# Attention probabilities turned by VectorE in 32x32 blocks, and a context product in four row tiles of 32 partitions

## The chip, the core and the metric

The kernel runs on one core of one Trainium2 chip. The metric is device time in microseconds, from the start to the end of one execution; of the kernel before there are three runs, and their median is what the prediction is compared with. A profiled execution gives every instruction's start, duration and releaser. Engines are named as in the profile: PE (matrix products; PEld is its weight load), DVE (VectorE), ACT (ScalarE), POOL (GpSimd) and SP, which here only issues transfers.

## The reference

The model is a gated two-layer block over x of 4 batches x 512 rows x 512. Layer 0 has a learned sparse adjacency over the context (top 153 of 512 per row) and a ternary feed-forward network behind a Hadamard transform. Layer 1 has the attention that this change touches, and a second ternary feed-forward network. The attention, cut to what matters (16 heads, 512 queries, 512 keys, latent width 128):

```python
q_big = rope(einsum('bshk,hkq->bshq', (hidden_q @ Wq.T), w_kc_q))
kv_r  = rope(kv_c)                                     # 512 x 128 per batch, for all heads
q_r   = einsum('bshq,hqr->bhsr', q_big, W_qr)
k_r   = einsum('bld,hdr->bhlr', kv_r, W_kr)
attn  = softmax(einsum('bhsr,bhlr->bhsl', q_r, k_r))   # 512 x 512 per head
ctx_c = einsum('bhsl,bld->bhsd', attn, kv_r)           # the context product
ctx   = einsum('bhsd,hkd->bhsk', ctx_c, w_kc_kv)       # folded with Wo into one matrix per head
out   = ctx @ Wo.T
```

## The kernel before

The kernel has three stretches. In the first (to about 286 us) it prepares the first batch's adjacency and feed-forward network, makes weights ternary, and `ahead` (lines 694-727) computes things for later: the rotated context `kv[b]` of every batch, which stays on chip as [128 keys of a chunk, 4 chunks, 128], and per head the folded matrix `om`, kept in DRAM. The middle stretch is `attention` (917-954): 4 batches x 8 pairs of heads, 32 pairs. In the last stretch the second feed-forward network of the last batch ends the kernel.

A pair runs in four quarters j = 0..3, one for each 128 queries. In a quarter, `scores(j)` makes for both heads the score tile [128 queries, 512 keys] (PE, lines 863 and 866, in 64 partitions each), its row maximum (DVE, 871), the exponentials with row sums (ACT, 874), the reciprocal (DVE, 876) and the normalized tile `pp` (ACT, 877). The next pair's queries are made in the same quarters: `head` (804), `rope` (819, with DVE 827, 829, 832 and POOL 833), and after the last quarter `rotated` (790, 792, in two column halves).

`turn(j)` (880-886) turns probabilities: for each head four PE transposes of 128x128 (885) into one PSUM bank `ppt`, then one ACT copy (886) into `pT`. It is called two quarters late, the last two after the quarters. Then `attended` (888-899) makes the context product: per head four accumulating products of `kv` (weights, 128 keys x 128) with `pT` (128 keys x 512 queries), and an ACT copy (898) to `cxo`. `added` (901-910) multiplies `cxo` with the two heads' `om` (905) for each 128 queries, and DVE adds the result to x (910). In fp32 the profile shows two PE instructions for each such product, and one for each transpose.

Other work is woven between the quarters. After each quarter, the loop at the end (1029-1051) takes steps of a list of jobs until their planned costs reach the share that is due: for batches 1 to 3 `before(b)`, which holds the adjacency of the next batch (the top-k by repeated MAX8, line 486, and MATCH_REPLACE8, line 491, on DVE), the keys of the next batch, and its first feed-forward network; in the last batch, the second network's weights and the second networks of batches 0 to 2. The top-k steps are given a priority 800 places behind (`high_priority(offset=-FILL)`, 483 and 488), so that they fill DVE where attention leaves room. Every engine works through its own list in a fixed order, made when the program is built; transfers are issued by SP and POOL, also in order.

PSUM has eight banks: four `mm` for products, two `tr` for transposes, two `bg` for the woven work. The on-chip tiles of this change are `pT` (two buffers of [128, 4, 512], one for each head), `pp` (seven), and `cxo` (three).

Of the kernel before, what the change touches and what calls it, by code (L numbers as in the profile page):

```python
# [9 lines left out]
F32 = mybir.dt.float32  # L10
# [24 lines left out]
def flamingo_kernel(  # L35
# [18 lines left out]
    wp = ctx.enter_context(tc.tile_pool(name="attn", bufs=2))  # L54
    ps = ctx.enter_context(tc.tile_pool(name="ps", bufs=4, space=bass.MemoryType.PSUM))
    pst = ctx.enter_context(tc.tile_pool(name="pst", bufs=2, space=bass.MemoryType.PSUM))
    psb = ctx.enter_context(tc.tile_pool(name="psb", bufs=2, space=bass.MemoryType.PSUM))

    def mm_ps(name):
        return ps.tile([P, 512], F32, tag="mm", name=name)  # L60

    def tr_ps(name):
        return pst.tile([P, 4, P], F32, tag="tr", name=name)


    alone = [True]
    turn_of = {"tr": 0, "big": 0, "front": 0}

# [10 lines left out]
    def bg_tr(name, dt=F32):  # L79
        if mine("tr", 4):  # L80
            return psb.tile([P, 4, P], dt, tag="bg", name=name)
        return pst.tile([P, 4, P], dt, tag="tr", name=name)

# [15 lines left out]

    lent = []  # L100

    def big(name):
        place = lent.pop(0) if lent else None
        if place == "h":
            t = hp.tile([P, NC, S], F32, tag="hT", name=name, bufs=1)
            return t.rearrange("p c s -> p (c s)")
        if place == "t":
            t = wp.tile([P, NT, S], F32, tag="pT", name=name)
            return t.rearrange("p j s -> p (j s)")
        if place == "b":  # L110
            return bp.tile([P, FF], F32, tag="big", name=name, bufs=3)
        turn_of["big"] += 1
        if not alone[0] or turn_of["big"] % 5 in (1, 3, 0):
            return bp.tile([P, FF], F32, tag="big", name=name, bufs=3)
        t = wp.tile([P, NT, S], F32, tag="pT", name=name)
        return t.rearrange("p j s -> p (j s)")

# [574 lines left out]
    spilled = {}  # L692

    def ahead():

# [7 lines left out]
        for b in range(B):  # L703
            cb = wp.tile([P, NT, DC], F32, tag="qh", name=f"cb_{b}")
            nc.gpsimd.dma_start(cb, cx[b * S : (b + 1) * S, :].rearrange("(j p) d -> p j d", p=P))
            t = const.tile([P, NT, DC], F32, tag=f"kv{b}", name=f"kv_{b}")
            nc.gpsimd.tensor_tensor(t, cb, cos_k, ALU.mult)
            rt = wp.tile([P, NT, DC], F32, tag="rs", name=f"rt_{b}", bufs=3)
            nc.gpsimd.tensor_tensor(rt[:, :, :hf], cb[:, :, hf:], sin_k[:, :, :hf], ALU.mult)
            nc.gpsimd.tensor_tensor(rt[:, :, hf:], cb[:, :, :hf], sin_k[:, :, hf:], ALU.mult)  # L710
            nc.gpsimd.tensor_tensor(t, t, rt, ALU.add)
            kv[b] = t
        yield
        for h in range(NH):
            wv = hp.tile([P, DC], F32, tag="wk", name=f"wv_{h}", bufs=3)
            nc.sync.dma_start(wv, wkckv[h])
            wo = wp.tile([P, D], F32, tag="rs", name=f"wo_{h}", bufs=3)
            nc.sync.dma_start(wo, woT[h])
            po = mm_ps(f"pO_{h}")
            nc.tensor.matmul(po, wv, wo, start=True, stop=True)  # L720
            om = wp.tile([P, D], F32, tag="cxo", name=f"oms_{h}", bufs=3)
            nc.scalar.copy(om, po)
            d = dram.tile([P, D], F32, tag=f"om{h}", name=f"omd_{h}")
            nc.gpsimd.dma_start(d, om)
            om_d[h] = d
            yield
        yield from keys(0)

    def keys(b):

        pt = bg_tr(f"pkv_{b}")
        for j in range(NT):
            nc.tensor.transpose(pt[:, j, :], kv[b][:, j, :], ident)

# [3 lines left out]
        for g in range(NG):  # L738
# [4 lines left out]
            if alone[0]:  # L743
                k = wp.tile([P, S], F32, tag="cxo", name=f"krs_{b}_{g}", bufs=3)
            else:
                k = front_t(f"krs_{b}_{g}")
# [47 lines left out]
    class Pair:  # L794
# [41 lines left out]
        def rotated(self):  # L836
# [5 lines left out]
            for o in range(3):  # L842
# [7 lines left out]
            nc.scalar.copy(self.qr, pr)  # L850
            self.pT = [
                wp.tile([P, NT, S], F32, tag="pT", name=f"pT_{u}_{i}") for i in range(2)
            ]

# [24 lines left out]

        def turn(self, j):  # L880
            for i in range(2):
                pt = tr_ps(f"ppt_{self.u}_{i}_{j}")
                pp = self.pps.pop((i, j))
                for l in range(NT):
                    nc.tensor.transpose(pt[:, l, :], pp[:, l * P : (l + 1) * P], ident)  # L885
                nc.scalar.copy(self.pT[i][:, :, j * P : (j + 1) * P], pt)  # L886

        def attended(self):
            self.cxo = []
            for i in range(2):  # L890
                pc = mm_ps(f"pc_{self.u}_{i}")
                for l in range(NT):
                    nc.tensor.matmul(  # L893
                        pc, kv[self.b][:, l, :], self.pT[i][:, l, :],
                        start=(l == 0), stop=(l == NT - 1),
                    )
                cxo = wp.tile([P, S], F32, tag="cxo", name=f"cxo_{self.u}_{i}", bufs=3)
                nc.scalar.copy(cxo, pc)  # L898
                self.cxo.append(cxo)

        def added(self):
            for j in range(NT):
                po = mm_ps(f"po_{self.u}_{j}")
                for i in range(2):
                    nc.tensor.matmul(  # L905
                        po, self.cxo[i][:, j * P : (j + 1) * P], self.oms[i],
                        start=(i == 0), stop=(i == 1),
                    )
# [8 lines left out]
    def attention(first):  # L917


        order = [(b, g) for b in range(B) for g in range(NG)]  # L920
        cur = first
        for at, (b, g) in enumerate(order):
            nxt = begin(*order[at + 1]) if at + 1 < len(order) else None
            cur.oms = out_weights(b, g)
            fresh = nxt is not None and nxt.b != b
            for j in range(NT):
                cur.scores(j)
                if nxt:
# [9 lines left out]
                    else:  # L938
                        nxt.rope(2)
                if j > 1:  # L940
                    cur.turn(j - 2)
                yield b, g
            cur.turn(NT - 2)
            cur.turn(NT - 1)
            if nxt:
                nxt.rotated()
            cur.attended()
            cur.added()
            if g == NG - 1 and b < B - 1:
                for j in range(NT):  # L950
                    d = dram.tile([P, D], F32, tag=f"xd{b}_{j}", name=f"xd_{b}_{j}")
                    nc.sync.dma_start(d, xs[b, j])
                    spilled[b, j] = d
            cur = nxt

# [34 lines left out]
    for _ in f0:  # L990
        step(early, 1)
    drain(early)
    hidden_T(0)
    first.head(0)
# [3 lines left out]
    first.rotated()  # L998
    alone[0] = False

    w1 = []
# [177 lines left out]
```

## Time and profile before

| | |
|---|---|
| runs of the kernel before | 2048.23, 2048.83, 2052.68 us; median 2048.83 us |
| span of the profiled execution | 2048.8 us |
| granted PE clock, mean over the span | 0.960 (0.77 in 0 to 286 us, 0.97 to 1.00 in attention) |
| PE / DVE / ACT / POOL busy | 1819.6 / 1630.3 / 1081.8 / 336.1 us |
| first score product, last `po` product | 286.3 us, 1961.4 us |
| attention batch 0 / 1 / 2 / 3 | 416 / 414 / 422 / 423 us |

The page gives, for each engine, its busy time and share of the span; then groups of equal instructions: line, engine, operation, tiles written and read, shape, count, busy time (overlaps counted once), mean duration of one, and the engine's idle time just before them. Tables by window give busy microseconds of each engine in a stretch of the span, with the number of instructions, and the granted PE clock. A timeline gives start, length, engine, line and operation; consecutive equal instructions are merged into one row with their count. Matrix products overlap in the pipeline, so the distance of two starts tells more than a duration.

### The profile page before, as it was taken

What the parts mean: (1) busy time and instruction counts of PE and PEld (TensorE: products, weight loads), DVE (VectorE), ACT (ScalarE), POOL (GpSimd) and SP (SyncE); (2) the same over time, 40 slices, a digit from 0 to 9 for tenths busy, and PEclk for the clock granted to TensorE, in tenths of its full rate; (3) what the DMA queues carried; (4) which work ended last, traced back from release to release, by engine and by line L of the source; (5) the groups of instructions that cost most, each with busy time, mean ns of one, the idle gap of its engine ahead of it and who ended that gap; (6) DMA issues with size and microseconds to landing.
All of it is one profiled execution on the core that took longest, in us unless ns stands there. A gap on an engine that the chain in (4) does not pass through costs nothing. (4 is left out here: it accounts for less than half of the span.)

```text
span 2048.8 us, 22947 instructions
## 1 busy us (share of the span) xinstructions
PE 1819.6 (89%) x7874; PEld 889.2 (43%) x7874; DVE 1630.3 (80%) x3305; ACT 1081.8 (53%) x1833; POOL 336.1 (16%) x316
## 2 busy tenths in 40 slices
PE   1268799999999999999999999999989999999898
PEld 0035534436554344455444444555443444444333
DVE  7989699987776999977778999778758556866785
ACT  6935454354434455453444564534786565555544
POOL 3020031123011122130111221301111210111000
PEclk6579899999999999999999999999999999999999
DMA  7451021111111222111122121111783112222011
GB/s 269 155 179 38 1 74 45 55 49 28 42 43 48 89 71 72 38 38 37 41 55 84 57 84 47 35 35 38 241 302 128 50 40 74 68 53 67 21 34 39
DMA packets 115556, 151.90 MB, mean 74 GB/s; under 512 B 57456, under 2 KB 68080, under 8 KB 112368
## 3 DMA queue, kind: packets, MB, share of 16 engines
q1 hardware_dynamic: 109968, 134.51, 22.0%
q0 software_dynamic: 4320, 14.16, 1.9%
q10 hardware_dynamic: 1152, 1.77, 0.2%
q8 instruction: 62, 1.02, 0.2%
q14 instruction: 54, 0.44, 0.1%
HBM read 117.90 MB, written 19.92 MB: 67 GB/s over the span
## 5 line engine op out<-in xcount | busy, mean ns | idle before, releaser
L833 POOL TENSOR_TENSOR ro<-ro,rs 128x512 f32<-128x512 f32 x192 | 255.4, 1333 | 1153.3 <-DVE rs L829 648.3
L874 ACT ACTIVATE pp<-pss,nm 128x512 f32<-128x512 f32 x256 | 174.6, 685 | 272.3 <-DVE nm L871 271.5
L804 PE MATMUL pqh<-hT,wq 128*128 128x512 f32 x512 | 239.7, 606 | 6.8 <-ACT pp L874 5.6
L893 PE MATMUL pc<-pT,kv 128*128 128x512 f32 x512 | 236.0, 600 | 2.7 <-ACT pT L886 2.6
L905 PE MATMUL po<-om,cxo 128*128 128x512 f32 x512 | 229.9, 597 | 0.0
L819 PE MATMUL pb<-qh,wc 128*128 128x512 f32 x384 | 189.4, 613 | 13.6 <-ACT qh L809 7.7
L486 DVE MAX8 m<-work 128x8 f32<-128x512 f32 x304 | 198.7, 684 | 0.6
L871 DVE TENSOR_REDUCE nm<-pss 128x1 f32<-128x512 f32 x256 | 167.8, 683 | 38.1 <-PE pss L866 37.9
L491 DVE MATCH_REPLACE8 work<-m,work 128x512 f32<-128x512 f32 x288 | 193.6, 678 | 0.1
L877 ACT ACTIVATE pp<-pp,rsm 128x512 f32<-128x512 f32 x256 | 178.6, 720 | 27.4 <-DVE rsm L876 26.2
L886 ACT COPY pT<-ppt 128x512 f32<-128x512 f32 x256 | 142.1, 588 | 38.5 <-PE ppt L885 38.0
L885 PEld LDWEIGHTS ppt<-ident,pp 128*128 128x128 f32 x1024 | 117.7, 142 | 96.6 <-issue 37.1
L885 PE MATMUL ppt<-ident,pp 128*128 128x128 f32 x1024 | 147.8, 279 | 10.1 <-ACT pp L877 4.4
L910 DVE SCALAR_TENSOR_TENSOR x<-po,gt,x 128x512 f32<-128x512 f32 x128 | 94.8, 745 | 68.4 <-PE po L905 67.6
L804 PEld LDWEIGHTS pqh<-hT,wq 128*128 128x128 f32 x512 | 93.1, 191 | 128.4 <-issue 89.6
L863 PE MATMUL pss<-kr,qr 64*128 64x512 f32 x256 | 143.4, 641 | 4.4 <-ACT pp L874 2.6
L905 PEld LDWEIGHTS po<-om,cxo 128*128 128x128 f32 x512 | 93.9, 190 | 119.5 <-issue 101.2
L866 PE MATMUL pss<-kr,qr 64*128 64x512 f32 x256 | 143.4, 641 | 0.7 <-DVE ro L827 0.5
L827 DVE TENSOR_TENSOR ro<-pb,cos_q 128x512 f32<-128x512 f32 x192 | 130.9, 682 | 10.3 <-PE pb L819 9.5
L893 PEld LDWEIGHTS pc<-pT,kv 128*128 128x128 f32 x512 | 91.9, 190 | 105.0 <-issue 90.4
L819 PEld LDWEIGHTS pb<-qh,wc 128*128 128x128 f32 x384 | 65.6, 189 | 113.6 <-issue 40.9
L898 ACT COPY cxo<-pc 128x512 f32<-128x512 f32 x64 | 37.4, 584 | 145.1 <-PE pc L893 144.8
(279 smaller groups left out, 3062.0 us busy)
## 6 DMA issues: line engine op xcount, KB each, us to landing
wq<-in_wqh SPq DMA_DIRECT2D x64, 256.0 KB, 2.7
om<-omd SPq DMA_DIRECT2D x64, 256.0 KB, 2.8
wc<-in_wkcq SPq DMA_DIRECT2D x32, 384.0 KB, 3.1
krd<-krs POOLq DMA_DIRECT2D x32, 256.0 KB, 2.5
kr<-krd SPq DMA_DIRECT2D x32, 256.0 KB, 2.7
sa_w1v<-in_gvT SPq DMA_DIRECT2D x8, 1024.0 KB, 5.3
sb_w1v<-in_gvT SPq DMA_DIRECT2D x8, 1024.0 KB, 5.2
wr<-in_wqr SPq DMA_DIRECT2D x32, 192.0 KB, 2.4
```

The costliest lines, as they stand in the source:

```text
L486: nc.vector.max(m8[j], cur[j])
L491: nc.vector.match_replace(works[j], m8[j], cur[j], GONE)
L804: nc.tensor.matmul(pq, self.wqs[i][:, c, :], hT[self.b][:, c, :], start=(c == 0), stop=(c == NC - 1),)
L819: nc.tensor.matmul(pb, self.wc[:, at : at + P], self.qhs[i if i < 2 else o], start=True, stop=True)
L833: nc.gpsimd.tensor_tensor(ro, ro, rs, ALU.add)
L863: nc.tensor.matmul(*args, start=True, stop=True)
L871: nc.vector.tensor_reduce(nm, pss[i], AX.X, ALU.max, negate=True)
L874: nc.scalar.activation(pp, pss[i], AF.Exp, bias=nm, accum_out=sm)
L877: nc.scalar.activation(pp, pp, AF.Copy, scale=rs)
L885: nc.tensor.transpose(pt[:, l, :], pp[:, l * P : (l + 1) * P], ident)
L893: nc.tensor.matmul(pc, kv[self.b][:, l, :], self.pT[i][:, l, :], start=(l == 0), stop=(l == NT - 1),)
L905: nc.tensor.matmul(po, self.cxo[i][:, j * P : (j + 1) * P], self.oms[i], start=(i == 0), stop=(i == 1),)
```

## The change

Probabilities are no longer turned on PE. `turn(j)` becomes two DVE instructions, one for each head: each turns the 32x32 blocks of a [128, 512] tile `pp` where they are, into `pT`. So row 32a+i of `pT` now holds key i of every block of 32 keys, for the 32 queries of block a. The keys of one block lie on 32 partitions in four copies (one for each 32 queries a), and the context product becomes, for each group a of 32 partitions, 16 accumulating products over the 16 blocks of 32 keys, with 256 columns (2 heads x 4 quarters x 32 queries). The four groups write four PSUM banks. The weights for this are the context laid out 32 rows at a time and repeated on all four groups: `kvrep`, loaded from DRAM for each batch by four transfers (`values`).

```diff
+    def values(b):
+        t = const.tile([P, 16, DC], F32, tag="kvrep", name=f"kvrep_{b}")
+        rows = kv_d[b].rearrange("(a i) j d -> i j a d", i=32)
+        for g in range(4):
+            nc.sync.dma_start(
+                t[32 * g : 32 * g + 32].rearrange("i (j a) d -> i j a d", j=NT), rows
+            )
+        kv[b] = t
...
         def turn(self, j):
+            if self.pT is None:
+                self.pT = wp.tile([P, 2, NT, S], F32, tag="pT", name=f"pT_{self.u}", bufs=1)
             for i in range(2):
-                pt = tr_ps(f"ppt_{self.u}_{i}_{j}")
-                pp = self.pps.pop((i, j))
-                for l in range(NT):
-                    nc.tensor.transpose(pt[:, l, :], pp[:, l * P : (l + 1) * P], ident)
-                nc.scalar.copy(self.pT[i][:, :, j * P : (j + 1) * P], pt)
+                nc.vector.transpose(self.pT[:, i, j, :], self.pps.pop((i, j)))
 
         def attended(self):
-            self.cxo = []
-            for i in range(2):
-                pc = mm_ps(f"pc_{self.u}_{i}")
-                for l in range(NT):
-                    nc.tensor.matmul(
-                        pc, kv[self.b][:, l, :], self.pT[i][:, l, :],
-                        start=(l == 0), stop=(l == NT - 1),
-                    )
-                cxo = wp.tile([P, S], F32, tag="cxo", name=f"cxo_{self.u}_{i}", bufs=3)
-                nc.scalar.copy(cxo, pc)
-                self.cxo.append(cxo)
+            pcs = [mm_ps(f"pc_{self.u}_{g}") for g in range(4)]
+            for c in range(16):
+                for g in range(4):
+                    rows = slice(32 * g, 32 * g + 32)
+                    with tc.high_priority() if c + g else nullcontext():
+                        nc.tensor.matmul(
+                            pcs[g][:, : 8 * 32], kv[self.b][rows, c, :],
+                            self.pT[rows, :, :, 32 * c : 32 * c + 32].rearrange("p i j s -> p (i j) s"),
+                            start=(c == 0), stop=(c == 15), skip_group_check=True,
+                        )
+            self.cxo = wp.tile([P, 8, 4, 32], F32, tag="cxo2", name=f"cxo_{self.u}", bufs=1)
+            for g in range(4):
+                nc.scalar.copy(self.cxo[:, :, g, :], pcs[g][:, : 8 * 32].rearrange("p (m s) -> p m s", m=8))
...
         for at, (b, g) in enumerate(order):
...
             for j in range(NT):
                 cur.scores(j)
...
-                if j > 1:
-                    cur.turn(j - 2)
+                if j == 0:
+                    if prev:
+                        ended(prev)
+                    cur.oms = out_weights(b, g)
+                cur.turn(j)
                 yield b, g
-            cur.turn(NT - 2)
-            cur.turn(NT - 1)
             if nxt:
                 nxt.rotated()
-            cur.attended()
-            cur.added()
...
-            cur = nxt
+            cur, prev = nxt, cur
+        ended(prev)
```

`ended(p)` calls `attended` and `added`, and at a batch's last pair spills x and calls `values(b + 1)`; it holds what stood at the end of the loop before. So product and addition of a pair stand in the first quarter of the next pair, behind that quarter's scores and query product. `high_priority` holds the 64 products of a pair together on PE.

Further edits: the two `tr` banks join `mm`, which now has six; `pT` is one tile for both heads with one buffer in place of two; `cxo` has one buffer, and the larger `cxo2` is new. `ahead` no longer keeps `kv[b]` on chip, it writes it to DRAM (four transfers on POOL's queue), and `keys(b)` loads it from there (one transfer on SP). Some tiles of the first stretch change their place (`oms`, `krs` in `ro`; the large tiles of `big` use the two halves of `pT`). `values(0)` stands ahead of the first pair.

## Prediction

> **What bounds the kernel now.** I read the busy shares first, then the busy time by stage, then the groups of the lines that go or move, then two stretches of the timeline. The chain of waits reaches back only to 1292 us and gives PE 23%, DVE 7%, ACT 4% of the span: PE leads, mostly with lines 893, 905, 436 and 804.
>
> The table by stage, split where the top-k of the next batch ends (columns: stage, its length, then busy us of each engine with instructions, granted PE clock, share of DMA, GB/s):
>
> ```profile
> core 0: us, PE busy (x) PEld busy (x) DVE busy (x) ACT busy (x) POOL busy (x), PEclk, DMA share, GB/s
> 286.00:452.00 166.00, 158.33 (x502) 67.89 (x502) 161.52 (x355) 80.99 (x162) 32.11 (x27) 1.00 0.17 50
> 452.00:702.00 250.00, 234.75 (x1286) 127.80 (x1284) 189.84 (x341) 111.49 (x210) 42.82 (x40) 0.99 0.17 44
> 702.00:876.00 174.00, 164.64 (x526) 71.54 (x526) 165.45 (x373) 89.31 (x174) 37.63 (x36) 1.00 0.23 69
> 876.00:1116.00 240.00, 228.17 (x1278) 124.19 (x1276) 186.71 (x334) 110.95 (x209) 43.20 (x36) 1.00 0.17 44
> 1116.00:1290.00 174.00, 164.45 (x523) 71.23 (x522) 165.47 (x372) 88.72 (x173) 37.66 (x36) 1.00 0.23 70
> 1290.00:1538.00 248.00, 230.13 (x1274) 127.78 (x1274) 179.74 (x302) 146.75 (x238) 44.19 (x36) 0.97 0.41 135
> 1538.00:1961.00 423.00, 400.92 (x1442) 175.56 (x1439) 286.00 (x576) 239.04 (x399) 54.53 (x42) 0.99 0.23 62
> ```
>
> Each of batches 0 to 2 has two stages of four pairs: a **top-k stage**, in which DVE is busy 95 to 97% and PE 95%, and a **feed stage**, in which PE is busy 93 to 95% and DVE 72 to 78%. Batch 3 (the last row) has no top-k: PE 95%, DVE 68%. So time taken from PE counts in the feed stages and in batch 3, and time added to DVE counts in the top-k stages. ACT is nowhere near the bound.
>
> What the change removes, and what it comes to sit beside, in the groups (columns: line, engine, operation, tiles, shape, count, busy us, mean ns, idle before with its releaser):
>
> ```profile
> L893 PE MATMUL pc<-pT,kv 128*128 128x512 f32 x512 | 236.0, 600 | 2.7 <-ACT pT L886 2.6
> ...
> L871 DVE TENSOR_REDUCE nm<-pss 128x1 f32<-128x512 f32 x256 | 167.8, 683 | 38.1 <-PE pss L866 37.9
> ...
> L886 ACT COPY pT<-ppt 128x512 f32<-128x512 f32 x256 | 142.1, 588 | 38.5 <-PE ppt L885 38.0
> ...
> L885 PE MATMUL ppt<-ident,pp 128*128 128x128 f32 x1024 | 147.8, 279 | 10.1 <-ACT pp L877 4.4 <-ACT pT L886 4.1 <-ACT hT L762 1.5
> ```
>
> **The PE transposes go.** 147.8 us busy and 10.1 us of waits before them, 157.9 us over 32 pairs: 4.9 us a pair off PE. The waits of the product for `pT` (2.7 us in all) go too; I leave them out.
>
> **The context product on PE.** Before, 16 PE instructions of 512 columns a pair; the chain shows sixteen in 7.06 us, and their starts lie 0.43 us apart, so 6.9 us. After, 64 products with two instructions each, 128 of 256 columns. At half of 0.43 us each, 27.5 us if they run one after the other, 6.9 us if four groups of partitions run beside each other. The nearest row is the score product, which already runs in two groups of 64 partitions (timeline of all engines, start and length):
>
> ```profile
> 1537.06 0.59 PE L905 MATMUL po<-om,cxo 128*128 128x512 f32 x1
> 1537.58 0.18 PEld L863 LDWEIGHTS pss<-kr,qr 64*128 64x128 f32 x1 [0.76 <-issue]
> 1537.58 0.69 PE L863 MATMUL pss<-kr,qr 64*128 64x512 f32 x1
> 1537.59 0.18 PEld L866 LDWEIGHTS pss<-kr,qr 64*128 64x128 f32 x1
> 1537.59 0.69 PE L866 MATMUL pss<-kr,qr 64*128 64x512 f32 x1
> ...
> 1538.11 0.59 PE L863 MATMUL pss<-kr,qr 64*128 64x512 f32 x1
> 1538.12 0.59 PE L866 MATMUL pss<-kr,qr 64*128 64x512 f32 x1
> ...
> 1538.64 0.70 PE L804 MATMUL pqh<-hT,wq 128*128 128x512 f32 x1
> ```
>
> The two heads start within 0.01 us of each other, weight loads too, although line 866 was issued behind both instructions of line 863. [...] The four instructions take 1.06 us, twice 0.43 us and 0.10 us at either end, where the array passes between whole and grouped: weights can't be loaded ahead there. Issue is no limit that this trace shows: the 1536 products of line 335 (128 columns, each with its weight load) fill 89.9 us from start to next start, 59 ns each, and 128 at that rate make 7.5 us. Bounds for the product: 6.9 us from above speed, 13.7 us if only the two groups that the trace shows run together, 27.5 us if none. I take four groups, 6.9 + 0.2 us, since the two that are shown run without loss. PE thus gains 4.9 - 0.2 = **4.7 us a pair**.
>
> [...] No row here has four groups.
>
> **DVE turns the tiles.** 8 instructions of 128x512 fp32 a pair, 256 in all; no row shows one. Every DVE row of that shape that reads one element at a time takes 0.67 to 0.69 us (lines 486, 491, 827, 871), the cheapest one-input row 0.58 us (184). Two merged ones take 1.28 us (line 871), so each costs 0.64 us of queue. From above: two passes, as a row of 1024 columns (line 588), 1.22 us. I take 0.64 us, the row that most resemble: 32 x 0.64 = 20.5 us in each stage of four pairs, 164 us in all.
>
> **What of it is on the path.** Top-k stages: DVE has 161.5, 165.5 and 165.5 us busy; with 20.5 us more, at 98% busy, they take 185.7, 189.8 and 189.8 us in place of 166, 174 and 174: **+51 us**. PE's gain is worth nothing there. Feed stages: PE gains 4 x 4.7 = 18.9 us in each; DVE reaches 210 us of 231, and below that in the other two, so PE still leads: **-57 us**. Batch 3: 8 x 4.7 = **-38 us**; DVE 286 + 41 = 327 us of 385.
>
> **Moved and cheap parts.** ACT loses 142.1 us (line 886), and its four half-size copies replace two: hidden, ACT is below 60% almost everywhere. All four copies now come at the end of the product, where before one of two was hidden; `po` waits for them, and PE has the next quarter's scores and `rope` to run. If that cover is gone, four copies at the 0.58 us of line 898, from above, cost 2.3 us a pair. With one `pT` buffer the first quarter's two DVE turns wait for the pair before to finish its product; behind them in DVE's order stand that pair's row maxima and rotation, and behind these PE and the top-k. The product stands 3.6 us of `pqh` and 7 us of its own behind the scores, about as long as row maximum, two exponentials and scaling take. Six `mm` banks less the four of the product leave two, which the scores need; with the trace's 1.3 us of reduce and 1.5 us of exponentials they come free in time. `values` puts 4 transfers on SP a batch, behind the last product, with `om` loads behind them that are due 30 us later; `keys` one load, `ahead` 4 stores on POOL: a transfer lands in 2.4 to 2.8 us by the page's rows. Hidden; at most 3 us each at the one exposed place, ahead of the first pair, and I put 1 us down for it.
>
> **Sum.** The span of 2048.8 us equals the median of the runs, so it needs no correction: 2048.8 + 51 - 57 - 38 + 1 = **2006 us**.
>
> **Rivals.**
>
> *The top-k slides into the feed stage* (it may lag 800 places). Then only the sum of DVE by batch counts: (351.4 + 41) / 0.98 = 400, 401 and 394 us for 416, 414 and 422, with PE's 376 to 384 below; -57 -38: 1954 us. For: DVE idles a quarter of the feed stage. Against: the feed network waits for the end of that top-k.
>
> *DVE waits more.* If turns that wait for ACT or PE bring DVE from 98 to 92% in top-k stages, these take 602 us, +88 in place of +51: 2043 us. For: DVE works in order, and the new wait for the product. Against: it now waits for ACT before each reciprocal (17 us in all) and is still 95 to 97% busy.
>
> *The turn takes two passes.* At 1.22 us, top-k stages grow by 108 us (492.5 + 117 at 98%, less 514), feed stages gain 16, 9 and 19 us, batch 3 38 us: 2075 us, **slower**. It decides from about 1.05 us a turn, where 92 us are lost and 91 gained. Against: all one-element rows lie near 0.68 us.
>
> *The product overlaps by two only*, 13.7 us, **slower** by +6.8 + 0.2 - 4.9 = +2.1 us a pair in the 20 pairs where PE leads: +43 + 51 = 2143 us. This is also the case in which the change doesn't do what it says. It decides from 9.2 us a pair, where PE's gain over 20 pairs (20 x 2.6) is no more than the 52 us lost elsewhere.
>
> **How the numbers follow.** Forecast 2006 us (own range 1985 to 2030) 0.40; sliding top-k (1950 to 1985) 0.15; DVE waits more (2030 to 2060) 0.17, split 0.06, 0.05, 0.06 between faster, same and slower; two passes (2060 to 2095) 0.13; two groups (2095 to 2150) 0.15. Faster by over 0.2%, about what a measurement of this kernel can tell from no change, 0.61; within it 0.05; slower 0.34. Leaving out the last rival and a little below gives 1955 to 2095 us.
>
> **What would show it.** Product: sixteen rounds of eight instructions at `pc` with four starts close together, and 7.1 us from first to last; 9 or 14 us mean lost overlap. Turns: a DVE row of 256 with a mean near 0.68 us. Top-k stages of 186 to 190 us with DVE at 98%, feed stages of 229 us, batch 3 in 385 us. DVE's idle before the turns, put down to `pc`, would speak for the second rival. The prediction is wrong if the top-k stages don't lengthen, or if PE doesn't gain in batch 3.

## The result, and the profile after

The change makes the kernel slower: 2361.05 us median (2357.63 to 2363.62, four runs) against 2050.76 us (2048.23 to 2053.5, four runs), a ratio of 1.1513 with a 95% interval of 1.1495 to 1.153. The profiled execution has a span of 2360.0 us, 311 us more than before.

The table by stage of the kernel after, cut at the same places of the work as the one before (columns as there):

```profile
core 0: us, PE busy (x) PEld busy (x) DVE busy (x) ACT busy (x) POOL busy (x), PEclk, DMA share, GB/s
322.00:547.00 225.00, 181.86 (x870) 89.19 (x870) 192.14 (x419) 71.62 (x149) 40.57 (x39) 0.87 0.13 39
547.00:839.00 292.00, 234.45 (x1587) 131.54 (x1588) 242.38 (x452) 106.48 (x198) 37.69 (x34) 0.90 0.17 44
839.00:1064.00 225.00, 182.85 (x1051) 94.29 (x1048) 162.69 (x351) 74.94 (x152) 42.78 (x42) 0.87 0.16 49
1064.00:1329.00 265.00, 213.65 (x1393) 115.69 (x1389) 225.97 (x415) 97.09 (x184) 34.87 (x30) 0.91 0.18 50
1329.00:1555.00 226.00, 182.90 (x1049) 94.42 (x1049) 163.75 (x356) 74.94 (x152) 42.79 (x42) 0.87 0.15 48
1555.00:1833.00 278.00, 221.91 (x1372) 125.42 (x1370) 184.05 (x290) 133.13 (x203) 31.54 (x24) 0.86 0.39 130
1833.00:2272.00 439.00, 393.75 (x2070) 184.49 (x2070) 312.59 (x627) 212.09 (x352) 55.22 (x42) 0.93 0.21 56
```

Every stage is longer, and none has a full engine: PE is busy 80 to 90% where it was 93 to 95%, DVE 66 to 85%. Before, one of the two was nearly always at work; now both wait, and the PE clock is down to 0.86 to 0.93 (0.97 to 1.00 before). The first score product comes at 322.1 us (286.3 before), batches take 517, 491, 504 and 439 us (416, 414, 422, 423), the end after the last `po` is unchanged (87.8 us). So 36 us are lost ahead of the attention and 275 us in it.

The groups that answer to those shown of before, and one that had hardly waited (`pr`, with its row of before in the second fence):

```profile
L909 PE MATMUL pc<-pT,kvrep 32*128 32x256 f32 x4096 | 284.1, 380 | 0.0
...
L901 DVE STREAM_TRANSPOSE pT<-pp 128x512 f32<-128x512 f32 x256 | 168.4, 690 | 109.4 <-PE pc L909 107.6 <-ACT pp L894 0.9
L888 DVE TENSOR_REDUCE nm<-pss 128x1 f32<-128x512 f32 x256 | 167.1, 680 | 66.4 <-PE pss L883 66.0
...
L809 PE MATMUL pr<-ro,wr 128*64 128x512 f32 x192 | 121.4, 733 | 139.6 <-POOL ro L852 139.0
```

```profile
L790 PE MATMUL pr<-ro,wr 128*64 128x512 f32 x192 | 99.1, 612 | 14.6 <-POOL ro L833 10.0 <-issue 3.9
```

The turn costs what one pass costs (690 ns; the row maximum 680). The product is 284.1 us over 32 pairs, 8.9 us a pair. New are the waits: DVE for the product to leave the one `pT` buffer (107.6 us), and PE for the sums `ro` that the rotation `pr` reads (139.0 us; 10.0 us before).

How a top-k pair goes wrong shows in the timeline of PE (first fence) and DVE (second) of the kernel after, in which the second pair's product began at 424.3 us:

```profile
447.86 0.59 PE L880 MATMUL pss<-kr,qr 64*128 64x512 f32 x1
447.87 0.59 PE L883 MATMUL pss<-kr,qr 64*128 64x512 f32 x1
455.85 4.09 PE L838 MATMUL pb<-qh,wc 128*128 128x512 f32 x4 [7.39 <-DVE x L927]
459.76 3.61 PE L823 MATMUL pqh<-hT,wq 128*128 128x512 f32 x8
```

```profile
452.02 1.28 DVE L489 MAX8 m<-work 128x8 f32<-128x512 f32 x2
453.22 1.29 DVE L901 STREAM_TRANSPOSE pT<-pp 128x512 f32<-128x512 f32 x2
454.43 0.71 DVE L500 SCALAR_TENSOR_TENSOR adj<-sim,m,sig 128x512 f32<-128x512 f32 x1
455.05 0.74 DVE L927 SCALAR_TENSOR_TENSOR x<-po,gt,x 128x512 f32<-128x512 f32 x1
...
459.73 1.28 DVE L888 TENSOR_REDUCE nm<-pss 128x1 f32<-128x512 f32 x2
```

PE had finished the pair's `po` at 447.4 us and stands 7.39 us for the first addition `x`, which has to free its bank. DVE isn't idle: from 423.2 us it does nothing but maxima and replacements of the next batch's top-k, 30 us in a row, because its list has them ahead of the addition. The row maxima of the scores at the top (459.73) come 11 us behind them. In the pairs 0, 1, 6, 7, 14 and 15 of the kernel after (counted from 0), 34 to 50 us of woven work (durations added up, turns not counted) stand between DVE's last row maximum, reciprocal or rotation and the first addition; in the same pairs of the kernel before, 6 to 14 us.

### The profile page after: what moved, and what is told of

Same layout as the page of the kernel before. It is cut to its first block, busy times and chain, and to the rows that moved or that the text cites. A ratio compares the mean times of both kernels' runs of the same rounds, so it can differ in the third digit from the quotient of the medians.

```text
span 2360.0 us, 28070 instructions
## 1 busy us (share of the span) xinstructions
PE 1851.9 (78%) x10434; PEld 958.3 (41%) x10434; DVE 1787.1 (76%) x3561; ACT 982.2 (42%) x1659; POOL 331.5 (14%) x320
## 4 chain that ended last, share of the span: by engine, by line
PE 42%; DVE 41%; ACT 8%; DMA 4%; issue 3%; POOL 2%; POOLq 0%; ACTq 0%; SPq 0%; DVEq 0%
PE po L923 7%; DVE work L494 7%; PE pc L909 7%; DVE m L489 7%; PE pqh L823 6%; DVE nm L888 3%; PE pss L880 3%; DVE rs L851 3%; DVE ro L846 3%; DVE pT L901 2%; PE pr L809 2%; PE pd_f L439 2%; POOL ro L852 2%; PE pd_g L439 2%; DVE rs L848 2%
## 5 line engine op out<-in xcount | busy, mean ns | idle before, releaser
L909 PE MATMUL pc<-pT,kvrep 32*128 32x256 f32 x4096 | 284.1, 380 | 0.0
L909 PEld LDWEIGHTS pc<-pT,kvrep 32*128 32x128 f32 x4096 | 254.2, 185 | 37.0 <-issue 13.0
L838 PE MATMUL pb<-qh,wc 128*128 128x512 f32 x384 | 198.6, 639 | 83.2 <-DVE x L927 73.4
L923 PE MATMUL po<-om,cxo 128*128 128x512 f32 x512 | 245.9, 633 | 19.8 <-ACT cxo L916 19.4
L823 PE MATMUL pqh<-hT,wq 128*128 128x512 f32 x512 | 257.7, 641 | 0.5 <-ACT hT L781 0.5
L901 DVE STREAM_TRANSPOSE pT<-pp 128x512 f32<-128x512 f32 x256 | 168.4, 690 | 109.4 <-PE pc L909 107.6
L809 PE MATMUL pr<-ro,wr 128*64 128x512 f32 x192 | 121.4, 733 | 139.6 <-POOL ro L852 139.0
L880 PE MATMUL pss<-kr,qr 64*128 64x512 f32 x256 | 159.8, 707 | 15.0 <-ACT qr L869 14.2
L883 PE MATMUL pss<-kr,qr 64*128 64x512 f32 x256 | 159.8, 707 | 0.0
L823 PEld LDWEIGHTS pqh<-hT,wq 128*128 128x128 f32 x512 | 101.2, 207 | 138.9 <-issue 124.9
L811 PE MATMUL pr<-ro,wr 128*64 128x512 f32 x192 | 121.4, 733 | 0.0
L916 ACT COPY cxo<-pc 128x256 f32<-128x256 f32 x128 | 39.5, 383 | 190.5 <-PE pc L909 190.5
```

The costliest lines, as they stand in the source:

```text
L823: nc.tensor.matmul(pq, self.wqs[i][:, c, :], hT[self.b][:, c, :], start=(c == 0), stop=(c == NC - 1),)
L838: nc.tensor.matmul(pb, self.wc[:, at : at + P], self.qhs[i if i < 2 else o], start=True, stop=True)
L880: nc.tensor.matmul(*args, start=True, stop=True)
L901: nc.vector.transpose(self.pT[:, i, j, :], self.pps.pop((i, j)))
L909: nc.tensor.matmul(pcs[g][:, : 8 * 32], kv[self.b][rows, c, :], self.pT[rows, :, :, 32 * c : 32 * c + 32].rearrange("p i j s -> p (i j) s" ...
L923: nc.tensor.matmul(po, cxo[:, NT * i + j, :], self.oms[i], start=(i == 0), stop=(i == 1))
```

## The experiments

The first theories were three: **W**, DVE waits for the one `pT` buffer, and what stands behind the waiting turn in its list comes late; **P**, the new place of product and addition; **B**, the shared banks. Later ones are **O**, the order of the engines' lists, **V**, the turns on DVE by themselves, and **R**, that TensorE has lost what it did while it waited. Times without an interval are of one run, with the kernel before at 2046.9 to 2047.9 us beside it (2052 us for those of e9 to e16). The sums of e5 to e9 and e14 are not the context, and e15 and e16 leave out most of the top-k.

**Which part of the change: place, buffer, banks.** Four kernels.

```diff
 e1: every turn one quarter later     -cur.turn(j)   +if j > 0: cur.turn(j - 1)
 e2: product at the end of its pair   -if prev: ended(prev)   +(after rotated) ended(cur)
 e3: two banks for transposes again   -bufs=6 (mm)   +bufs=4 (mm), bufs=2 (tr)
 e4: kernel before, product and addition moved to the next pair's first quarter, nothing else
```

> The changed kernel with every DVE turn one quarter later, so that the first turn of a pair no longer stands in DVE's order ahead of the product that must free pT. Theory W (the wait of DVE for the single pT buffer, 107.6 us in 17 waits): about 2250 us, and no waits of the turns for pc. Theory P (place: product and addition, 14 us of PE in one piece ahead of the pair's second quarter, make PE and DVE work in turns): the waits go but little time, 2310 to 2350 us. Theory B (banks: transposes and products share one list of banks that is given out in order): no change, 2340 to 2370 us.

> The changed kernel with product and addition back at the end of their own pair, as before the change; turns by DVE and the four row groups stay. Theory P: 2000 to 2080 us, the granted clock back at 0.94 or more. Theory W: 2200 to 2260 us, since the turns no longer wait for pc but nothing else changes. Theory B: 2300 us or more.

> The changed kernel with two PSUM banks of their own for the remaining transposes and four for products, as before the change. Theory B: the first score product back from 322 us to about 286 us and attention shorter by 100 us or more, 2100 to 2200 us. Theories P and W: the first stretch back at 286 us, attention as it is or longer (the product takes all four banks), 2320 to 2400 us.

> The kernel before with one part of the change alone: product and addition moved to the first quarter of the next pair, behind its scores and query product; turns by PE, old product, old banks. pT is free in time, since turns start two quarters later. Theory P: 2150 to 2300 us, with PE waiting for POOL's ro. Theories W and B: 2030 to 2070 us.

Measured: e1 2343.24, e2 2336.51, e3 2366.8, e4 2122.5 us. Turning later leaves DVE's wait for `pc` where it was (108.8 us), so e1 does not test W. In e2 no turn waits for `pc` any more, and W had it at 2200 to 2260 us. The place costs 75 us in the kernel before, yet taking it back gives only 25 here. With banks of their own for transposes the first score product comes at 294.6 in place of 322.1 us, but the batches take 535, 495, 505 and 449 us. None of W, P and B is the bulk.

**Whose instructions: product or turn.** In e5 and e6 the 64 products over 32 partitions become 16 over all 128, four to each bank; e7 and e8 put turns back or move only them.

```diff
 e5 (place of the change), e6 (end of the pair)
-for c in range(16): for g in range(4): matmul(pcs[g], kv[32*g:32*g+32, c], pT[32*g:32*g+32, ..., 32c:32c+32])
+for g in range(4): for c in range(4*g, 4*g+4): matmul(pcs[g], kv[:, c], pT[:, ..., 32c:32c+32])
 e7 = e2 with   +nc.tensor.transpose(...) x4; nc.scalar.copy(self.pT[:, i, :, j*P:(j+1)*P], pt)
 e8 = before with   +nc.vector.transpose(self.pT[i][:, j, :], pp)   for transposes and copies
```

> The changed kernel with its product as 16 products over all 128 partitions (256 columns each, four into each of the four banks) in place of 64 over 32 partitions; what the blocks sum to is no longer the context, the work left on every engine and the copies are the same. Theory O (each engine's order was fixed with the four row groups counted one after another, so VectorE gets some 20 us a pair too much of top-k and normalisation ahead of the additions): the product keeps its 7 us, but VectorE's work between its last attention instruction and the first addition falls from 35 to 50 us to about 15 in most pairs, and the time to 2060 to 2150 us. Theory W (VectorE waits for the one pT buffer) and theory P (the place): no change in the product's length, so 2330 to 2370 us. A fourth, that row groups hold up TensorE in a way the trace does not show: 2060 to 2150 us as well, but with VectorE's work between the two points unchanged at 35 to 50 us.

> The same product over all 128 partitions (again not the context) in the version with product and addition at the end of their own pair, which took 2336.5 us. Theory O: VectorE's work between the last attention instruction and the first addition falls from 38 us to about 15, and the time to 2030 to 2100 us, below that of the same product in the next pair's first quarter by the 25 to 75 us that the place costs. Theories W and P, and theory B (banks): 2310 to 2340 us.

> The version with product and addition at the end of their own pair (2336.5 us), its turns put back to TensorE and ScalarE (whole 128x128 transposes, so that what the row groups then sum is not the context), its product left as four row groups. Theory O: VectorE loses 164 us of turns, but the order still counts the four row groups one after another, so 35 to 50 us of other VectorE work stay ahead of the first addition in most pairs and the time stays at 2200 us or more. Theory V (the 164 us of turns on VectorE are the cause, whatever the order): back to 2050 to 2100 us.

> The kernel before with one part of the change: the probabilities turned by VectorE in 32x32 blocks into the old tiles, the old product over 128 partitions at its old place (blocks are turned only within themselves, so the context is not the right one); TensorE's transposes and ScalarE's copies of them go. Theory O: the order is planned with the right durations, so only the work moved counts: VectorE gains 164 us, TensorE loses 158, and the time comes out at 2010 to 2070 us. Theory V: VectorE's turns alone bring most of the loss, 2200 us or more.

Measured: e5 2205.65, e6 2201.12, e7 2411.72, e8 2114.33 us. The form of the product alone is worth 155 us (e5), though TensorE needs hardly longer for 23 of the 32 products of the kernel after (7.3 to 7.9 us) than for those of e5 (7.1 us). In e5 the woven work ahead of the first addition is 10 to 13 us in twelve of the fourteen pairs that have top-k there (24 to 25 us in pairs 6 and 14), near what theory O said; the time stays 56 us above its range. Theory V falls as the main cause: with the 164 us of turns taken off DVE again the kernel is slower still (e7), and the turns alone cost 67 us (e8). In e8 undisturbed pairs do become shorter, 36 us for 40 to 45, but the top-k gets less room beside them: in the first batch it ends at 484 us (439 before), and the feed network behind it at 698 us (650). PE has no more attention to do by then, and a batch's last pair takes 88 to 137 us (47 to 52 before), with 88.8 us of waits in all in the feed network's last product, alone now, for its operands. What the pairs gain is given back at the border: batches 0 to 2 take 86 us more together, and batch 3, which has no such border, 20 us less (403.5 us). e8 flatters the turn besides: its product over a chunk of keys reads only one quarter's turn, the real one reads all four.

**Setting the order by hand.** e9 takes e6 and traces the product ahead of `pr`; e10 to e12 keep the 64 products and bind the woven work behind the last addition.

```diff
 e9, e11, e12   +cur.attended()   ahead of nxt.rotated()
 e10 to e12     -FILL = 800   +FILL = 0
                +with tc.issue_after(marks["x"].ins): spent += next(gen)
 e12            +two of the six banks only for transposes until the attention starts
```

> As the run with the product over all 128 partitions at the end of its own pair (2201.1 us; the sums are not the context), but the product traced ahead of the next pair's rotation pr, so that TensorE has the product to do while GpSimd ends the sums ro that pr reads. Theory R (the undivided product leaves TensorE nothing to do while it waits for ro, 5.7 us in a quiet pair; in the kernel before half the product stood between the parts of pr): the wait of pr for ro falls from 125 us to under 40, quiet pairs from 43 to 45 us to 37 to 40, and the time to 2080 to 2140 us. Rival: the wait moves to pc, which then waits for the last turn on VectorE; 2180 to 2220 us.

> The changed kernel's own product, 64 products over 32 partitions, at the end of its own pair (2336.5 us so far), with one thing changed in the order: what is traced of the next batch's normalisation, top-k and feed stage is queued on VectorE behind the last addition x of the pair before, and the top-k is no longer put 800 places back in priority. Theory O (it is the order and not the row groups): 12 to 23 instructions in place of 55 to 66 between the last attention instruction and the first addition, and 2180 to 2240 us, near the product over 128 partitions at the same place (2201.1 us). Rival (row groups cost of themselves): 2300 us or more.

> Both of the two runs before: order of VectorE bound to the additions, and the product of 64 ahead of pr. If theories O and R add up: 2080 to 2160 us. If the order alone does it and the wait only moves: 2180 to 2240 us.

> As the run with bound order and the product ahead of pr, with two of the six banks kept for transposes until the attention starts and shared by all from then on (every third tile). Theory B (in the first stretch the transposes and products of successive row tiles wait for each other in the shared banks): first score product at 285 to 296 us in place of 320, and the time 24 to 36 us below that of the run before it. Otherwise no change of the first stretch.

Measured: e9 2219.42, e10 2494.46, e11 2633.47, e12 2895.25 us (ratio 1.412, 1.4096 to 1.4144). Theories O, R and B missed. In e9 the wait for `ro` goes and one for the turn comes, 87.7 us of `pc` for `pT`: the rival. In e10 the DVE work ahead of the addition is down to 4 to 20 us in the first two batches, as wanted, but the top-k that was there now stands between row maxima, rotation and turns, and PE waits 218.0 us for `ro`. And the order inside the product had changed: from first to last it takes 7.7 us at best and 14.5 us often in e10, and 25.9 us (median) in e12, where the first score product comes at 305.8 us (333.6 in e11), later than theory B had it. PE's list says why. The four groups of partitions, by number, of one pair's 64 products:

```
after, pairs 0 and 1   0102132132132132132132132132132132132132132132130230000000000000   13.9 and 13.2 us
after, pair 5          0102132132132013201320132013201320132013201320132013201320132030   7.3 us
e12, pair 9            1212121212121212121212121212121203030303030303030303030303030303   26.1 us
```

In these lists groups overlap only where they alternate (7.3 us in pair 5). Where three alternate, the fourth runs by itself and takes another 5.6 to 7.0 us (six long pairs of the kernel after, some of it at half the clock); by twos, pair 9 of e12 takes 26.1 us with the clock at half (starts 0.43 us apart for 0.21), an estimated 13 us at the full one. So e10 to e12 can't be held for or against theory O.

**Carrying a whole order over.** In e13 the changed kernel's own instructions are queued, on all five engines, in the order made for e5; in e14 those of e5 in the order of the changed kernel. e15 and e16 repeat before and e13 with a top-k that reads 16 columns of 512.

```diff
 e13, e14   +for every engine: each instruction is queued behind the one before it in the other kernel's list
 e15, e16   -nc.vector.max(m8[j], cur[j])   +nc.vector.max(m8[j], cur[j][:, :16])   (match_replace likewise)
```

> The changed kernel instruction for instruction, its 64 products over 32 partitions included, but queued on all five engines in the order that was made for the version with 16 products over all 128 partitions in the same place (the 64 stand together where the last of those 16 stood). Theory O (of the 313 us lost, the part between 2205.7 and 2361 us is the order that was made with four row groups counted one after another): 2190 to 2230 us. Rival G (the row groups cost that much themselves on the chip, whatever the order): 2330 to 2380 us.

> The reverse: the 16 products over all 128 partitions (sums that are not the context, the same work otherwise) queued on all five engines in the order of the changed kernel. Theory O: 2330 to 2370 us. Rival G: 2190 to 2230 us.

> The kernel before with its top-k cut short: each of the 624 maxima and replacements reads 16 columns of 512, so VectorE loses some 350 us of filler (the cut is not the one wanted, all else is done). Theory D (VectorE is what paces the top-k stages of before and after): batches 0 to 2 fall from 414 to 421 us to about 385 to 400, paced by TensorE, batch 3 stays within 5 us of 423.8. It is the base for the next run.

> The changed kernel with the same short top-k, in the order made for products over 128 partitions (as in the first run of this call). Theory D (VectorE has no room for the turns beside the top-k; with room they pay): quiet pairs 35 to 38 us, below those of the kernel before with the short top-k, batches 0 to 2 at 365 to 385 us. Rival S (the turn stands in the chain from scores to product, so TensorE waits for it even when VectorE has room): quiet pairs 41 us or more, batches no shorter than those of the run before this one.

e13 takes 2243.31 us (ratio 1.0928, 1.0899 to 1.0957), e14 2333.04 us. The same instructions are 118 us faster in the other order, and e5's are 127 us slower in this one: **the order is shown**, and rival G falls. Of the 118 us, 52 lie in the product itself, whose groups rotate strictly in e13; e14's product has no groups. The groups of e13:

```profile
L932 PE MATMUL po<-om,cxo 128*128 128x512 f32 x512 | 235.3, 607 | 28.4 <-ACT cxo L925 28.4
L918 PE MATMUL pc<-pT,kvrep 32*128 32x256 f32 x4096 | 232.1, 377 | 0.1
...
L818 PE MATMUL pr<-ro,wr 128*64 128x512 f32 x192 | 120.3, 724 | 135.6 <-POOL ro L861 134.9
```

The product now takes 7.2 us in every pair but three (7.9 there); e5's takes 7.1 us. Of the 38 us left between e13 and e5, 31 lie between the first product and the first `po`, 6 of them in the products and 25 behind them: e13 has 8.5 us there in quiet pairs, e5 7.5, since four groups in step end together and all four ACT copies follow (28.4 us of waits for `cxo`, 8.6 in e5).

The busy times of e15:

```profile
PE 1818.6 (89%) x7874; PEld 885.1 (43%) x7874; DVE 1336.5 (65%) x3305; ACT 1101.8 (54%) x1849; POOL 331.1 (16%) x316
```

e15 takes 2046.16 us: taking some 290 us off DVE (1336.5 us busy for 1630.3) changes nothing. Batches are 412, 412, 421 and 427 us. Theory D falls: **DVE did not pace the top-k stages of the kernel before**, in spite of its 95 to 97%; its filler only filled. e16 takes 2184.46 us, batches 458, 437, 448 and 431 us: rival S. That is 59 us below e13, so room on DVE does count after the change, as it did not before it; 138 us above e15 remain. The way from its third pair to its fourth, on PE, and the same stretch by windows:

```profile
431.76 1.16 PE L577 MATMUL pza_f<-had_sb,hT_f 128*128 128x128 f32 x8
438.45 1.11 PE L818 MATMUL pr<-ro,wr 128*64 128x512 f32 x1 [5.53 <-POOL ro L861]
...
441.14 1.22 PE L889 MATMUL pss<-kr,qr 64*128 64x512 f32 x1 [0.71 <-ACT qr L878]
...
442.15 1.06 PE L889 MATMUL pss<-kr,qr 64*128 64x512 f32 x1
```

```profile
424.90:438.40 13.50, 8.02 (x30) 3.05 (x28) 12.82 (x28) 5.44 (x12) 7.79 (x8) 0.87 0.22 68
438.40:446.00 7.60, 6.83 (x13) 2.14 (x14) 2.68 (x8) 2.46 (x6) 0.00 (x1) 0.56 0.09 26
446.00:463.30 17.30, 16.59 (x157) 10.35 (x155) 3.56 (x5) 3.18 (x8) 0.00 (x0) 1.00 0.05 16
```

There is no top-k here, yet in 424.9 to 438.4 us DVE is busy 12.82 of 13.50 us, with row maxima, reciprocals, rotation and turns until 437.2 us, while PE has 8.02 us to do. One of the two pairs of turns stands ahead of the last rotation, which it puts off by 1.2 us. Then PE runs at a clock of 0.56, and in 446 to 463 us DVE has 3.56 us of work. **What binds is a stretch of each pair, not a stage**: scores, maxima, rotation, turns, product follow each other, and a turn lengthens DVE's share of just that stretch. Without the transposes PE waits in it (134.9 us for `ro` in e13), unless other work stands there (in e8 half of the product does, and `pr` waits 15.7 us for `ro` in all). In the kernel before the transposes stood there, as its timeline in a quiet pair shows:

```profile
772.63 0.59 PE L790 MATMUL pr<-ro,wr 128*64 128x512 f32 x1
...
773.16 1.09 PE L885 MATMUL ppt<-ident,pp 128*128 128x128 f32 x8
774.18 0.64 PE L790 MATMUL pr<-ro,wr 128*64 128x512 f32 x1
...
775.19 7.13 PE L893 MATMUL pc<-pT,kv 128*128 128x512 f32 x16
```

(What the expectation of e9 says of half a product between the parts of `pr` holds for e8, and for five of the 32 pairs of the kernel before.)

**Cover, and the banks.**

```diff
 e17 = e2, the product in two halves (quarters 0 and 1 ahead of pr, 2 and 3 behind it),
       DVE, ACT, POOL and SP in the order of the same halves over 128 partitions
 e18 = before with   -bufs=4 (mm), bufs=2 (tr)   +bufs=6 (mm)
```

> The changed kernel's turns and row-group products at the end of their own pair, the product in two halves: 64 products of 128 columns for the row tiles 0 and 1, which TensorE has to do ahead of the rotation pr, and 64 for the row tiles 2 and 3 behind it; VectorE, ScalarE, GpSimd and SyncE in the order made for the same halves over 128 partitions. Theory R (the transposes taken away, and the half product that stood between the parts of pr, had filled the time in which TensorE waits for the sums ro; now it waits, and runs slower for some us after it): the wait of pr for ro falls from 135 us to under 50 us, quiet pairs to 37 to 41 us, and the time to 2110 to 2180 us. Rival T (the wait is for VectorE as such, and only changes its name): waits of pc for pT take its place, and 2200 to 2250 us.

> The kernel before with one part of the change: the two banks of the transposes given to the common pool of six. Theory B (the sharing sets successive row tiles of the first stretch one behind the other): first score product at 310 to 322 us in place of 286, batches 0 to 3 within 10 us each, and 2070 to 2090 us in all. Otherwise 2040 to 2060 us.

e18 takes 2069.81 us (ratio 1.0088, 1.0073 to 1.0104). The first score product moves from 286 to 315.9 us, the four batches together gain 10 us: of the 36 us lost ahead of the attention, 30 are the shared banks. e17 takes 2415.46 us (1.1786, 1.1766 to 1.1806), a miss. The wait for `ro` does fall to 28.0 us, and where the groups are in step pairs are down to 38 to 40 us (pairs 0, 1, 24 and 25), as theory R said; but PE's list, which was not carried over here, takes the groups by twos in many halves, and other quiet pairs take 41 to 51 us. Its border pairs take 110 to 150 us, long as in e8. That cover would bring the rest back isn't shown by a total.

## Why the prediction was wrong

The result splits into a chain of kernels, each one step from the next (of one run where no interval is given above):

| step | from, to (us) | |
|---|---|---|
| DVE turns in the kernel before (e8) | 2046.9 to 2114.3 | +67 |
| one undivided product that needs all turns, in the next pair's first quarter, one `pT`, shared banks (e5) | to 2205.7 | +91 |
| four row groups in the same order, copies at the end (e13) | to 2243.3 | +38 |
| the order made for four row groups | to 2361.1 | +118 |

The second step is not taken apart. By themselves the banks cost 20 us in the kernel before (e18), and the place 5 us (e5 against e6); that the rest, some 66 us, is the undivided product with its waits is argued and not shown.

**The step that failed first** is "what of it is on the path". It took the engine that is busiest in a stage for the one that paces it, so that PE time taken from feed stages would be gained whole (-57, -38) and DVE time added to top-k stages would cost +51. e15 shows the second premise wrong for the kernel before, where DVE's 95 to 97% was filler. Adding to DVE does cost, but not where the sum had it: in e8 the top-k pairs get shorter, and the time is lost in a batch's last pair, behind a late top-k. In e8 PE's gain does come in batch 3, 20 of the 38 us. e13 and e16 show that it is not gained whole beside the new product: the 4.9 us a pair that left PE came back as waits for `ro` (134.9 us in e13 against 10.0) and as a slower clock (mean over the span 0.895 in e13 against 0.960; 0.56 behind such a wait in e16). Stages of 186 to 190 and 229 us and a last batch of 385 us were forecast; 225, 265 to 292 and 439 us came.

**The second** is "moved and cheap parts", which took for granted that every engine's list stays as it is. It is made anew with the change. Around the 64 products it puts 24 to 26 us more of woven DVE work ahead of the additions than e13's, in each of the six pairs named above, not far from the 20 us between 27.5 us for groups one after another and 7 us together; and it lets groups fall apart (284.1 us of product in all, 232.1 in e13). That the list is planned with groups one after another fits both and is not shown; that the list is worth 118 to 127 us is (e13, e14).

Term by term. *Transposes go, 157.9 us:* they went, as above. *Product 7.1 us a pair:* right in size, 7.2 us in e13, but not by whatever list PE has: after the change it is 7.3 us at best, 12.6 to 14.3 us in six pairs and 8.9 us in the mean. *Turns 0.64 us of queue:* right, two take 1.29 us (the cheapest one-input row is 0.54 us, in other groups of line 184, and not 0.58; nothing hangs on it). *Copies hidden:* wrong; in quiet pairs the first `po` starts 1.3 us behind the end of the product in e13, 0.5 us in e5 and at once in the kernel before; the text had 2.3 us a pair for cover gone. *One `pT` buffer hidden:* wrong in the kernel after (107.6 us of DVE waits; 47.5 us in e13), but e2, in which no turn waits for `pc`, gains 25 us only, so it is mostly the lateness of the product that is seen there. *First stretch +1 us:* +36, of them 30 the banks (e18), a term that I had not looked for in that stretch at all. *The place:* taken as free; +75 us in the kernel before (e4), 5 us between e6 and e5.

*Rivals.* Each needed one engine full; none came. "DVE waits more" had the right direction (DVE is busy 76% of the span), but was priced at 2043 us. Two passes (1.22 us a turn) and overlap by two only (13.7 us) are ruled out by 0.69 us a turn and by the 7.2 us of e13, though products by twos do occur where the list says so (e12, e17).

## What to carry to other kernels

Before work is moved from one engine to another, follow one round of the loop in the timeline and mark which engine waits for which inside it: time taken from the fuller engine is worth something only where it isn't waiting for the other one, and DVE at 95%, busy with filler, did not pace its stage here (2046 us in e15 without most of the filler, 2052 us with it). Where the build fixes each engine's order, a change of an instruction's form can change that order everywhere (118 us here); carry the old order over, or count what stands between two dependent instructions, before blaming the instruction. In these runs groups of partitions ran beside each other only as long as they alternated in PE's list (7.2 us with all four in step, 12.6 to 14.3 us with the fourth by itself).

## What the runs showed of the hardware

**The clock at half, behind a wait and behind one group.** In the timeline of the kernel after, at the rotation and the next scores:

```profile
414.87 0.64 PE L809 MATMUL pr<-ro,wr 128*64 128x512 f32 x1 [2.41 <-POOL ro L852]
...
417.06 1.22 PE L880 MATMUL pss<-kr,qr 64*128 64x512 f32 x1 [0.70 <-ACT qr L869]
...
418.07 1.06 PE L880 MATMUL pss<-kr,qr 64*128 64x512 f32 x1
419.06 5.26 PE L823 MATMUL pqh<-hT,wq 128*128 128x512 f32 x8
```

Behind the wait of 2.41 us the granted clock is at half from 415.4 to 422.2 us (1.00 in 413.0 to 415.4 us), so it had fallen before the wait of 0.70 us. Scores take 1.22 and 1.06 us for 0.69 and 0.59, the query product 5.26 us for 3.6.

It also fell without any wait. In the first pair of the kernel after, three groups alternate until 363.7 us, and then the fourth runs by itself (windows; the PE clock is the third column from the end):

```profile
356.70:364.20 7.50, 7.50 (x107) 7.13 (x107) 7.50 (x19) 0.83 (x2) 0.00 (x0) 1.00 0.14 37
364.20:367.60 3.40, 3.40 (x18) 2.91 (x17) 3.40 (x10) 0.68 (x3) 0.00 (x0) 1.00 0.00 0
367.60:370.60 3.00, 3.00 (x8) 1.84 (x6) 3.00 (x9) 0.00 (x0) 0.00 (x0) 0.50 0.00 0
```

PE has an instruction running all the time from 350.3 to 370.6 us, and yet the clock is at half from 367.6 us: starts lie 0.43 us apart for 0.22. Pairs 1, 22 and 23 have the same list of groups and show the same: in the four pairs the clock was at half from 4.0, 4.7, 5.3 and 4.9 us after the fourth group began to run by itself, and at 1.00 for the 6.9 us in which three alternated. With two in turn, the product of pair 9 of e12 ran at half the clock; whether that came of its groups is open.

**Four groups in step.** 128 instructions of 256 columns took 7.2 us in e13, about as long as the 32 over 128 partitions of e5 (7.1 us).

**Loads where the form changes.** The 0.10 us that the prediction puts at either end of the scores stand in the kernel before: there load and product start together (1537.58 us; the product takes 0.69 us for 0.59), while the load of the last `po`, behind others of its form, starts 0.43 us ahead of its product (1537.06 us):

```profile
1536.63 0.19 PEld L905 LDWEIGHTS po<-om,cxo 128*128 128x128 f32 x1 [0.24 <-issue]
```
